# Delta-rule layer: output normalization gathered in the last slots, look-ahead of eleven slots in place of twelve

## The chip, the cores and the metric

The kernel runs on one core of a Trainium2 chip. Its engines are TensorE (PE, with its weight loads as PEld), VectorE (DVE), ScalarE (ACT), GpSimd (POOL) and SyncE (SP), which issues all the transfers spoken of here. The metric is the device time of one execution in microseconds (us); lower is better.

## What is computed

The reference is a chain of eight layers on a tensor x of shape 4 x 1024 x 128 (float32); each adds its result to x after a layer norm of its input. Only the first layer is touched, a delta rule with 8 heads of 16 dimensions:

```python
q = (x @ Wq).reshape(Bb, Ll, H, HD);  k = (x @ Wk).reshape(Bb, Ll, H, HD)
k = k / jnp.maximum(jnp.linalg.norm(k, axis=-1, keepdims=True), 1e-12)
v = jax.nn.silu(x @ Wv).reshape(Bb, Ll, H, HD)
beta = jax.nn.sigmoid(x @ Wb)
def step(S, inp):                       # over the 1024 tokens
    qt, kt, vt, bt = inp
    Sk = jnp.einsum('bhk,bhkv->bhv', kt, S)
    S = S + jnp.einsum('bh,bhk,bhv->bhkv', bt, kt, vt - Sk)
    ot = jnp.einsum('bhk,bhkv->bhv', qt, S)
    return (S, ot)
S0 = jnp.zeros((Bb, H, HD, HD), x.dtype)
_, os_ = jax.lax.scan(step, S0, (qs, ks_, vs, bs))
o = jnp.moveaxis(os_, 0, 1).reshape(Bb, Ll, Dd)
mu = jnp.mean(o, axis=-1, keepdims=True);  var = jnp.var(o, axis=-1, keepdims=True)
return (o - mu) / jnp.sqrt(var + 1e-05) * ln_w + ln_b
```

## The kernel before

`l0_attn` cuts the 1024 tokens into 32 chunks of 32 tokens (NS = 32, C = 32). A chunk holds the tokens of all four batches, so that its 4 x 32 rows fill 128 partitions. Within a chunk the recurrence is solved in closed form; from chunk to chunk a state S is carried. After a first part (layer norm and projections, which ends 49 us into the span) the work goes through a list of *slots* written out by hand: the loop `for slot in range(-LAG - 1, NS + 4)` issues, for chunk c = slot, a fixed sequence, and `tc.manual_schedule()` keeps that order on every engine. Each engine works through its own list in order; semaphores alone tie the lists together.

In slot c these steps are issued, in this order:

- the state applied to the chunk: matmuls into `up`, then ACT copies it to `ux` (L426, four instructions) and `uP` (L428);
- `gram(c + LAG)`: 8 pairs of Gram matmuls into `wide` (L277), ACT copies them to `kk` (L301), SP stores the diagonal blocks to DRAM (`ld`, L304), and for each fourth chunk SP loads the whole group of four chunks back as `L` (L307);
- `fetch(c + 2)`: SP loads the solved matrices `tb` from DRAM (`td`, L330);
- `root` (L396): the square root of an output tile's variance, on ACT;
- the state update: matmuls into `sp` (L437), ACT copies to the next `S` (L445);
- in two slots of four, one half of `query` for the next group (matmul L337, copy L341);
- `apply(c + 1)`: matmuls with `tb` into `wp` (L349), ACT copies to `wu` (L354);
- the first half of this slot's share of `solve`;
- the output matmuls `oT` (L457), ACT copy `ot`;
- `attend(c + 2)`: score matmuls into `wide` (L277) and on DVE one multiply with the causal mask, `mt<-wide,upper` (L366);
- the output: matmuls into `op`, ACT copy `o` (L474), SP stores it to DRAM as `od` (L475);
- `flip(c + LAG + 1)`: two POOL multiplies (L283, L284), four transposes (L288), two ACT copies `kt` and `bt` (L292, L294);
- the second half of this slot's share of `solve`;
- `reload`, `moments` and `norm` of an output tile, where one is due.

`solve(n)` is a forward substitution over a group of four chunks at a time (n = 0 to 7), on DVE: 31 steps of two instructions each (L319 `pr<-T,L`, L322 `T<-T,pr`), cut by PARTS into eight parts, two for each of four slots. `T` starts as a copy of `eye` on POOL (L313); after part 7 SP stores T to `td` (L324).

An output tile n is 128 tokens of all four batches, four chunks. `reload(n)` (SP load `on<-od` at L381, and on POOL the addition of `ln_b` to x at L382), `moments(n)` (on DVE 4 x `bn_stats` L390 and `bn_aggr` L391), `root(n)` and `norm(n)` (on DVE a reciprocal L401 and 4 x two fused instructions, L403 and L405) come four to seven slots after the tile's first chunk: `every(k)` gives the tile n in slot 4n + k, and is asked with 4, 6, 7 and 7. So before the change the DVE work of tile n falls into the slots 4n + 6 and 4n + 7, and LAG = 12 sets how far `flip`, `gram` and `solve` run ahead: with `n = (slot + 7) // 4` the four parts of solve(n) lie in the slots 4n - 7 to 4n - 4.

Two things tie DVE and PE to each other in each slot. The score matmuls of `attend` and the Gram matmuls both write `wide`, and the mask multiply reads it: the Gram matmuls of the next slot wait for this slot's mask multiply. And DVE, working in order, starts a mask multiply only after the solve instructions issued ahead of it.

Of the kernel before, what the change touches and what calls it, by code (L numbers as in the profile page):

```python
# [9 lines left out]
F32 = mybir.dt.float32  # L10
# [5 lines left out]
P = 128  # L16
NB, SEQ, D = 4, 1024, 128
TPB = SEQ // P
# [9 lines left out]
class Net:  # L28
# [112 lines left out]
    def l0_attn(self):  # L141
# [6 lines left out]
        nc, tc = self.nc, self.tc  # L148
        wkvb, wq, ln_w, ln_b = self.l0
        H, HD, C = 8, 16, 32  # L150
        NS, LAG = SEQ // C, 12
        PARTS = (0, 7, 11, 14, 16, 18, 21, 25, 31)
        mm = nc.tensor.matmul
        tok = self.xnT.rearrange("p (c r) -> p c r", r=P)
        with ExitStack() as c_:
            one = c_.enter_context(tc.tile_pool(name="dn1", bufs=1))
            two = c_.enter_context(tc.tile_pool(name="dn2", bufs=2))
# [55 lines left out]
            def heads(a):  # L213
                return a.rearrange("p (h d) -> p h d", h=H)
# [4 lines left out]
            with tc.tile_pool(name="dnl", bufs=NB) as ln, tc.tile_pool(name="dnp", bufs=3, space=PSUM) as pp_, tc.tile_pool(  # L219
                name="dnx", bufs=2, space=PSUM  # L220
# [76 lines left out]
            def gram(c):  # L297
                kt, bt = kT[c]
                sc = score(kt, bt, 0)
                kk = two.tile([P, H, P], F32, tag="kk", name="kk")  # L300
                nc.scalar.copy(kk.rearrange("p (j g) t -> p j g t", g=2), sc)  # L301
                for b in range(NB):
                    r = slice(C * b, C * b + C)
                    nc.sync.dma_start(ld[c, b].rearrange("h s t -> s h t"), kk[r, :, r])  # L304
                if c % 4 == 3:
                    Ls[c // 4] = L = two.tile([P, C, C], F32, tag="L", name="L")
                    nc.sync.dma_start(L, ld[c - 3 : c + 1].rearrange("c b h s t -> (c b h) s t"))  # L307
# [18 lines left out]
            def fetch(c):  # L326
                tb = tbs[c % len(tbs)]
                for b in range(NB):
                    r = slice(C * b, C * b + C)
                    nc.sync.dma_start(tb[r, :, r], td[c, b].rearrange("h s t -> s h t"))  # L330
# [26 lines left out]
            def with_state(out, w, g):  # L357

                for b in range(NB):
                    r = slice(C * b, C * b + C)  # L360
                    mm(out[r, g, :], lhsT=w[:, g, r], rhs=Ss[c % 2][:, g, b, :], start=True, stop=True)

            def attend(c):
                sc = score(kT[c][0], qs[c // 4][:, c % 4], 1)
                mt = two.tile([P, H, P], F32, tag="mt", name="mt", bufs=3)
                nc.vector.tensor_mul(  # L366
                    mt.rearrange("p (j g) t -> p j g t", g=2), sc,
                    upper.unsqueeze(1).unsqueeze(2).to_broadcast([P, 4, 2, P]),
                )
                del kT[c]  # L370
                return mt
# [3 lines left out]
            def of(n):  # L375
                return self.x.rearrange("p (b t) d -> p t b d", b=NB)[:, n]

            def reload(n):

                o = two.tile([P, NB, D], F32, tag="on", name="on")  # L380
                nc.sync.dma_start(o, od[:, n * P : (n + 1) * P, :].rearrange("b p d -> p b d"))  # L381
                nc.gpsimd.tensor_add(of(n), of(n), ln_b.unsqueeze(1).to_broadcast([P, NB, D]))  # L382
                outs[n] = [o]

            def moments(n):
                o = outs[n][0]
                mv = two.tile([P, NB, 2], F32, tag="mv", name="mv")
                for b in range(NB):
                    st = two.tile([P, 6], F32, tag="st", name="st", bufs=4)
                    nc.vector.bn_stats(st, o[:, b, :])  # L390
                    nc.vector.bn_aggr(mv[:, b, :], st)  # L391
                outs[n].append(mv)

            def root(n):
                rs = two.tile([P, NB], F32, tag="rs", name="rs")
                nc.scalar.activation(rs, outs[n][1][:, :, 1], AF.Sqrt, bias=self.eps)  # L396
                outs[n].append(rs)

            def norm(n):
                o, mv, rs = outs.pop(n)  # L400
                nc.vector.reciprocal(rs, rs)  # L401
                for b in range(NB):
                    nc.vector.scalar_tensor_tensor(o[:, b, :], o[:, b, :], mv[:, b, 0:1], ln_w, ALU.subtract, ALU.mult)  # L403
                    xs = of(n)[:, b, :]
                    nc.vector.scalar_tensor_tensor(xs, o[:, b, :], rs[:, b : b + 1], xs, ALU.mult, ALU.add)  # L405
# [3 lines left out]
            def every(k):  # L409

                n = (slot - k) // 4
                return (n,) if (slot - k) % 4 == 0 and 0 <= n < NS // 4 else ()

            for slot in range(-LAG - 1, NS + 4):
                c, part = slot, (slot + 7) % 4
                n = (slot + 7) // 4
                cut = (2 * part, 2 * part + 1) if 0 <= n < NS // 4 else ()
                if 0 <= c < NS:
                    mt = late.pop(c)
                    up = psm.tile([P, 2, 64], F32, tag="sm", name="up")  # L420
                    for g in range(2):
                        with_state(up, wus.pop(c) if g else wus[c], g)

                    ux = two.tile([P, 2, NB, 64], F32, tag="ux", name="ux")
                    for b in range(NB):
                        nc.scalar.mul(ux[:, :, b, :], up, nbb[:, b : b + 1])  # L426
                    u = ups[c % 2]
                    nc.scalar.mul(u[:, :, 0:HD], heads(up.rearrange("p g d -> p (g d)")), -1.0)  # L428
                if 0 <= c + LAG < NS:
                    gram(c + LAG)  # L430
                if 0 <= c + 2 < NS:
                    fetch(c + 2)
                for i in every(7):
                    root(i)
                if 0 <= c < NS:
                    for g in range(2):
                        mm(  # L437
                            sp[:, g].rearrange("p a b -> p (a b)"),
                            lhsT=kns[c % len(kns)][:, 4 * g : 4 * g + 4, :].rearrange("p a b -> p (a b)"),
                            rhs=ux[:, g].rearrange("p a b -> p (a b)"), start=False, stop=True, skip_group_check=True,  # L440
                        )
                    if c + 1 < NS:
                        for j in range(4):
                            r, d = slice(32 * j, 32 * j + HD), slice(HD * j, HD * j + HD)
                            nc.scalar.copy(Ss[(c + 1) % 2][r, :, :, d], sp[r, :, :, d])  # L445
                for g in range(2):
                    for i in every(g - 4):
                        query(i, g)
                if 0 <= c + 1 < NS:
                    wus[c + 1] = apply(c + 1)  # L450
                for i in cut[0:1]:
                    solve(n, i)
                if 0 <= c < NS:
                    oT = psm.tile([P, 2, P], F32, tag="sm", name="oT")
                    for g in range(2):
                        for j in range(4):
                            mm(  # L457
                                oT[32 * j : 32 * j + 32, g, :], lhsT=u[:, 4 * g + j, :], rhs=mt[:, 2 * j + g, :],
                                start=True, stop=True,
                            )  # L460
                    ot = two.tile([P, 2, P], F32, tag="ot", name="ot")
                    nc.scalar.copy(ot, oT)
                if 0 <= c + 2 < NS:
                    late[c + 2] = attend(c + 2)
                if 0 <= c < NS:
                    op = psm.tile([P, 2, 64], F32, tag="sm", name="op")
                    for g in range(2):
                        with_state(op, qs[c // 4][:, c % 4], g)
                        mm(
                            op[:, g, :], lhsT=ot[:, g, :], rhs=pick.rearrange("p j v -> p (j v)"),  # L470
                            start=False, stop=True, skip_group_check=True,
                        )
                    o = two.tile([P, D], F32, tag="o", name="o")
                    nc.scalar.copy(o, op.rearrange("p g d -> p (g d)"))  # L474
                    nc.sync.dma_start(od[:, c * C : (c + 1) * C, :], o)  # L475
                if 0 <= c + LAG + 1 < NS:
                    flip(c + LAG + 1)
                for i in cut[1:]:
                    solve(n, i)
                for i in every(4):  # L480
                    reload(i)
                for i in every(6):
                    moments(i)
                for i in every(7):
                    norm(i)

# [1169 lines left out]
```

## Time and profile before

| what | us |
|---|---|
| median of six runs (2816.16 to 2829.55) | 2821.89 |
| the profiled execution, its own time | 2817.83 |
| its span, first to last instruction | 2816.1 |
| first solve instruction (L319) on DVE | 69.6 |
| last solve instruction on DVE, slot 24 | 321.4 |
| first mask multiply (L366), slot -2 | 104.0 |
| last mask multiply, slot 29 | 349.7 |
| last chunk's output copied (L474), slot 31 | 364.5 |

The span is the time on the core; the execution's own time lies 1.7 us above it. The stretch of slots thus covers about the first eighth of the span; the seven layers behind it are not touched. In the trace a group of instructions has its busy time, the mean of one, and the idle time of the engine before it with what ended it. "A <- B" among waits means that A's engine sat idle until B ended.

### The profile page before, as it was taken

The page shows a single profiled execution, that of the slowest core. Times are in us where ns is not written, and L with a number is a line of the kernel's source. Part 1 is how long each engine was busy: PE and PEld are TensorE (multiplying, and loading weights), DVE is VectorE, ACT ScalarE, POOL GpSimd, SP SyncE. Part 2 cuts the span into 40 slices and gives each one's busy share as a digit, 9 for nine tenths or more (in the row PEclk, how much of TensorE's full clock was granted, in tenths as well). Part 3 has the DMA queues.
Part 4 walks back from the last instruction along what each step waited for, and adds up shares of the span by engine and source line. Part 5 has one row for each costly group of instructions (what it writes and reads, how often), then busy time and mean ns, then how long its engine had stood idle before and what let it go on. Part 6 is the DMA issues. An engine that isn't in the chain of part 4 may idle for free.

```text
span 2816.1 us, 51848 instructions
## 1 busy us (share of the span) xinstructions
PE 2552.0 (91%) x20320; PEld 1282.5 (46%) x20320; DVE 1831.1 (65%) x3857; ACT 1537.4 (55%) x3486; POOL 179.5 (6%) x301
## 2 busy tenths in 40 slices
PE   5678768999989959999999768999999999999977
PEld 4455535699985523333333343333333333333356
DVE  5999657467763666777676146777776776777134
ACT  4465466655554450665666650666666666666642
POOL 6111000000000000000000050000000000000001
PEclk8698868899998965999999865999999999999968
DMA  2233220000000000000100000000000000000000
GB/s 53 63 86 77 55 59 1 1 1 1 2 2 1 1 1 15 13 14 14 21 14 10 5 0 8 8 8 11 9 9 9 8 12 8 10 8 8 4 9 24
DMA packets 116468, 46.62 MB, mean 17 GB/s; under 512 B 88402, under 2 KB 110843, under 8 KB 116220
## 3 DMA queue, kind: packets, MB, share of 16 engines
q1 hardware_dynamic: 116220, 43.25, 7.8%
q8 instruction: 163, 2.67, 0.4%
q14 instruction: 85, 0.70, 0.1%
HBM read 16.95 MB, written 12.98 MB: 11 GB/s over the span
## 4 chain that ended last, share of the span: by engine, by line
PE 63%; DVE 3%; ACT 2%; POOL 1%; issue 1%; DMA 0%; SPq 0%; POOLq 0%; DVEq 0%; ACTq 0%
PE pb L1183 30%; PE po L1205 15%; PE pa L1158 6%; PE ep L975 2%; PE tp L120 2%; PE pp L1098 1%; PE gp L923 1%; PE bp L988 1%; DVE st L82 1%; ACT xn L109 1%; PE pv L1079 1%; PE op L617 0%; PE bp L986 0%; DVE mv L83 0%; PE rp L1576 0%
## 5 line engine op out<-in xcount | busy, mean ns | idle before, releaser
L1187 ACT ACTIVATE es<-pb 128x512 f32<-128x512 f32 x1536 | 836.2, 594 | 561.2 <-PE pb L1183 406.6
L1183 PE MATMUL pb<-q,k 32*128 32x512 f32 x3072 | 957.5, 642 | 0.7 <-ACT es L1187 0.7
L1158 PE MATMUL pa<-k,q 32*128 32x512 f32 x3072 | 913.2, 680 | 16.8 <-DMA q<-q 15.9
L1170 DVE TENSOR_REDUCE bm<-pa 128x2 f32<-128x1024 f32 x512 | 626.1, 1225 | 275.4 <-PE pb L1183 169.4
L1205 PE MATMUL po<-es,v 128*32 128x256 f32 (+1 forms) x5760 | 480.0, 405 | 0.0
L1183 PEld LDWEIGHTS pb<-q,k 32*128 32x128 f32 x3072 | 314.7, 184 | 347.4 <-ACT es L1187 189.0
L1166 DVE TENSOR_REDUCE bm<-pa 128x16 f32<-128x1024 f32 x256 | 312.7, 1222 | 107.3 <-PE pb L1183 60.6
L1205 PEld LDWEIGHTS po<-es,v 128*32 128x32 f32 x5760 | 114.2, 108 | 543.1 <-issue 510.5
L1158 PEld LDWEIGHTS pa<-k,q 32*128 32x128 f32 x3072 | 253.7, 193 | 94.4 <-DVE bm L1170 50.4
L120 PE MATMUL tp<-ident,xn 128*128 128x128 f32 x192 | 65.3, 439 | 56.3 <-ACT xn L109 50.5
L319 DVE TENSOR_TENSOR pr<-T,L 128x31 f32<-128x31 f32 (+15 forms) x248 | 91.5, 369 | 27.6 <-DMA L<-ld 20.6
L1212 DVE COPY oT<-po 128x512 f32<-128x512 f32 x48 | 32.8, 682 | 109.1 <-PE po L1205 109.1
L322 DVE TENSOR_TENSOR T<-T,pr 128x31 f32<-128x31 f32 (+15 forms) x248 | 92.5, 373 | 8.5
L109 ACT ACTIVATE xn<-x,nm,rs 128x128 f32<-128x128 f32 x224 | 89.4, 482 | 7.6 <-DVE nm L106 7.6
L984 DVE SCALAR_TENSOR_TENSOR x<-ep,g,x 128x128 f32<-128x128 f32 x160 | 55.2, 349 | 30.0 <-ACT sc L982 19.9
L120 PEld LDWEIGHTS tp<-ident,xn 128*128 128x128 f32 x192 | 34.4, 186 | 88.3 <-ACT xn L109 60.0
L277 PE MATMUL wide<-bt,kt 32*128 32x128 f32 x512 | 32.7, 387 | 45.6 <-DVE mt L366 29.6
L729 ACT ACTIVATE w<-tr,half 128x128 f32<-128x128 f32 x128 | 47.0, 367 | 48.0 <-PE tr L727 45.1
L82 DVE BATCH_NORM_STATS2 st<-x 128x6 f32<-128x128 f32 x256 | 65.3, 266 | 11.8 <-DMA x<-in_L_attn_x_dram 3.9
L704 ACT ACTIVATE a<-hp,wb 128x128 f32<-128x128 f32 x128 | 47.0, 367 | 40.9 <-PE hp L700 39.9
L975 PE MATMUL ep<-L_ffn_expert_w,xnT 128*128 128x512 f32 x128 | 68.4, 624 | 0.0
L1457 POOL MEMSET c<- 128x512 f32 (+1 forms) x2 | 2.3, 1171 | 1021.7 <-PE tp L120 1021.7
(442 smaller groups left out, 3570.4 us busy)
## 6 DMA issues: line engine op xcount, KB each, us to landing
ld<-kk SPq DMA_DIRECT2D x128, 32.0 KB
L<-ld SPq DMA_DIRECT2D x8, 512.0 KB
td<-T SPq DMA_DIRECT2D x8, 512.0 KB
tb<-td SPq DMA_DIRECT2D x128, 32.0 KB
md<-nt SPq DMA_DIRECT2D x192, 2.0 KB
q<-md SPq DMA_DIRECT2D x192, 2.0 KB
x<-in_L_attn_x_dram SPq DMA_DIRECT2D x4, 512.0 KB
od<-o SPq DMA_DIRECT2D x32, 64.0 KB
```

Of the source, the lines that this page charges most:

```text
L82: nc.vector.bn_stats(st, src[:, i, :])
L109: nc.scalar.activation(dst[:, i, :], src[:, i, :], AF.Identity, bias=nm[:, i : i + 1], scale=rs[:, i : i + 1])
L120: nc.tensor.transpose(tp[:, i, :], xn[:, 4 * q + i, :], self.ident)
L319: nc.vector.tensor_mul(pv, T[:, 0 : j + 1, j : j + 1].to_broadcast(sh), L[:, j : j + 1, j + 1 :].to_broadcast(sh))
L322: nc.vector.tensor_sub(T[:, 0 : j + 1, j + 1 :], T[:, 0 : j + 1, j + 1 :], pv)
L975: nc.tensor.matmul(ep.rearrange("p a b -> p (a b)"), lhsT=self.tok(t), rhs=ew[:, 4 * h : 4 * h + 4, :].rearrange("p a b -> p (a b)"), star ...
L1158: nc.tensor.matmul(pa[:, j % 2, :], lhsT=st["q"][r, i * P : (i + 1) * P], rhs=st["k"][r, n * 512 : (n + 1) * 512], start=True, stop=True,)
L1166: nc.vector.tensor_reduce(out[:, :, 1:9], pa.rearrange("p j (c s) -> p j c s", c=8), axis=AX.X, op=ALU.max)
L1170: nc.vector.tensor_reduce(out[:, :, n : n + 1], pa, axis=AX.X, op=ALU.max)
L1183: nc.tensor.matmul(pb, lhsT=st["k"][r, kc * P : (kc + 1) * P], rhs=st["q"][r, n * 512 : (n + 1) * 512], start=True, stop=True,)
L1187: nc.scalar.activation(es[turn][:, j, :], pb, AF.Exp, scale=scale)
L1205: nc.tensor.matmul(po[r, cols], lhsT=vring[b % 2][:, kc, 4 * g + j, :], rhs=es[:, j, cols], start=kc == 0, stop=True, skip_group_check=True,)
```

## The change

It moves the output steps of the tiles 0 to 6 from every fourth slot into consecutive slots at the end, and sets LAG to 11. `reloads` lists the slots of `reload`: 23 to 29 for the tiles 0 to 6, and 32 for tile 7; `moments` come one slot later, `root` and `norm` two slots later. The buffers `on` and `mv` get three copies in place of two. With LAG = 11 each `flip`, `gram` and `solve` part is issued one slot later as counted from its chunk: solve(n) lies in the slots 4n - 6 to 4n - 3. The ring `kn` and the buffers `kt` are one smaller (LAG + 3). The loop runs from slot -12 to 34 in place of -13 to 35.

```diff
-        NS, LAG = SEQ // C, 12
+        NS, LAG = SEQ // C, 11
...
-                o = two.tile([P, NB, D], F32, tag="on", name="on")
+                o = two.tile([P, NB, D], F32, tag="on", name="on", bufs=3)
...
-                mv = two.tile([P, NB, 2], F32, tag="mv", name="mv")
+                mv = two.tile([P, NB, 2], F32, tag="mv", name="mv", bufs=3)
...
-            for slot in range(-LAG - 1, NS + 4):
-                c, part = slot, (slot + 7) % 4
-                n = (slot + 7) // 4
+            reloads = [NS - TPB - 1 + i for i in range(TPB - 1)] + [NS]
+            for slot in range(-LAG - 1, NS + 3):
+                c, part = slot, (slot + 6) % 4
+                n = (slot + 6) // 4
...
-                for i in every(7):
-                    root(i)
+                if slot - 2 in reloads:
+                    root(reloads.index(slot - 2))
...
-                for i in every(4):
-                    reload(i)
-                for i in every(6):
-                    moments(i)
-                for i in every(7):
-                    norm(i)
+                if slot in reloads:
+                    reload(reloads.index(slot))
+                if slot - 1 in reloads:
+                    moments(reloads.index(slot - 1))
+                if slot - 2 in reloads:
+                    norm(reloads.index(slot - 2))
```

## Prediction

> **What bounds the kernel now.** I read the slices of the page first, then busy time by stretch, then DVE's waits, then DVE's timeline.
>
> ```profile
> PE   5678768999989959999999768999999999999977
> DVE  5999657467763666777676146777776776777134
> ```
>
> Each digit is 70 us. Only in slices 2 to 4 (70 to 281 us) is DVE the full engine, and there lie the slots. Elsewhere PE leads, and the change does not reach it. By stretch (window, its length, busy time and instruction count of PE, PEld, DVE, ACT, POOL, granted clock):
>
> ```profile
> 69.60:321.40 251.80, 192.75 (x2816) 133.70 (x2816) 231.92 (x608) 133.27 (x405) 33.41 (x50) 0.80 0.32 71
> 321.40:364.50 43.10, 34.03 (x549) 23.79 (x548) 13.83 (x39) 20.55 (x74) 0.00 (x0) 0.83 0.22 51
> ```
>
> DVE is busy 92% from the first solve instruction to the last, 32% after it. Its waits between 69 and 322 us:
>
> ```profile
> DVE pr L319 <- DMA L<-ld: 20.6, 1, 20.6
> DVE mt L366 <- PE wide L277: 2.8, 4, 1.4
> ```
>
> The first ended at 69.6. So in 252 us DVE waited 2.8 us: there the slots run at DVE's pace, and what leaves DVE there can shorten them, until PE and ACT lead. The next lines are DVE's, then POOL's (start, length):
>
> ```profile
> 131.65 1.37 DVE L319 TENSOR_TENSOR pr<-T,L 128x247 f32<-128x247 f32 x1
> ...
> 260.52 1.28 DVE L322 TENSOR_TENSOR T<-T,pr 128x175 f32<-128x175 f32 x1
> 261.73 1.21 DVE L366 TENSOR_TENSOR mt<-wide,upper 128x1024 f32<-128x1024 f32 x1
> 263.24 1.31 DVE L322 TENSOR_TENSOR T<-T,pr 128x192 f32<-128x192 f32 x1
> ...
> 260.26 4.07 POOL L382 TENSOR_TENSOR x<-x,L_attn_ln_b 128x512 f32<-128x512 f32 x3
> ```
>
> A solve instruction that runs beside POOL's addition of ln_b takes 1.3 us, 0.95 more than its like (0.42, 0.34 and 0.36 us). The mask multiply beside it keeps its 1.21.
>
> **The change part by part.** I write M(s) for the start of the mask multiply of slot s. In the trace M(2) = 135.0, M(6) = 166.9, M(10) = 201.0, M(14) = 234.8, M(18) = 269.7, M(22) = 301.2, M(25) = 323.3, M(29) = 349.7.
>
> *Norms leave.* One tile costs DVE 169.78 to 171.38 (moments) and 177.13 to 180.03 (norm), 4.5 us; tiles 1 to 4 cost 4.3 to 4.4. Five tiles lay ahead of 321.4: 21.7 us leave the full stretch. That is a gain only where DVE then still leads.
>
> *What is late next.* Between two mask multiplies DVE has 4+4, 6+8, 12+14 or 8+6 solve instructions: undisturbed 3.6, 5.8, 7.7 to 8.0 and 6.0 us, each plus 1.14 for the mask. PE's price is from the end of a mask multiply, which frees `wide`, to the end of the next scores. In slot 6 (159.29 to 162.89) it is 3.6 at full clock; in slot 10 (193.34 to 199.66) 6.3 at half. With the first half of a query it is 6.3 in slot 4, with the second 5.7 in slot 5; both at full clock, but starting 0.9 late from ACT's copies.
>
> LAG = 11 moves the solve parts one slot on: 4+4 falls into slots 0 mod 4, where the query makes PE slow, 6+8 into slots 1, 12+14 into slots 2, 8+6 into slots 3. One group of four slots after the change, mask to mask:
> - slot 3: DVE leads, 1.14 + 6.0, plus 0.7 for POOL's copy of `eye` (the copy at 133 us lengthened one solve instruction from 0.42 to 1.13) and 0.2 for the flip: 8.0;
> - slot 0: PE leads. Nearest rows 4.5 (slot 9, a query with `wide` just freed) to 6.3 (slot 4); slot 4 lost 0.4 of it to a late `tb` behind the L load, which moves to slot 1. I take 5.0: 1.22 + 5.0 = 6.2;
> - slot 1: PE leads, U + 4.86 as in slot 5 (151.15 to 156.01), where U, the start of `ux`, comes 2.2 after the scores. The L load now stands before its `tb`: from `kk` (137.2) to the use of `tb` (147.1) it took 10 us in slots 3 and 4, which here ends about 0.6 after the 5.8 of the U path. 1.22 + 6.4 = 7.6;
> - slot 2: DVE leads, 1.14 + 8.0: 9.1.
>
> Sum 30.9; a half clock in slot 0 or 1 adds 1 to 2 and shows in two of three groups before, mostly where DVE covers it. I take 31.5, bounds 30 to 34. Before, it was 33.7 (134.7 over four groups).
>
> *The stages.*
> 1. Up to slot 2. DVE starts solving at 69.6 as before: L comes from the same four Gram chunks. M(-2) now stands behind 62 + 14 solve instructions, not 90; that point was passed at 98.1, M(-2) was 104.0. Then 1.14 + 6.0, then 1.22 + 6.6 (PE's row of slot 0, at half clock), then 7.6 and 9.1: M(2) = 98.1 + 7.1 + 7.8 + 7.6 + 9.1 = 129.7. Gain 5.3.
> 2. Slots 3 to 18: 4 x 31.5 = 126.0, plus 1.6 in slot 18 (item 3), against 134.7. Gain 7.1.
> 3. Slots 19 to 22. POOL's eight additions were spread; now the built order has them in a row behind the last copy of `eye`, which waits for the store of T(5). That is M(17) + 1.1 + 3.5 + 3.1 (the last store of this kind was issued at 256.1, the copy started at 259.25), just ahead of M(18). Eight times 1.43 us from there: one addition and the copy hit slot 18 (1.6), one runs beside a mask multiply, six hit slot 19: 1.14 + 6.0 + 5.7 = 12.8. Slots 20 to 22: 7.2, 7.3, 8.8. Sum 36.1 against 31.5. Loss 4.6.
> 4. Slots 23 to 25: 7.1; 5.8 (PE); 1.14 + 2.6 + 1.6 + 3.2 = 8.5 (six solve instructions, moments(0), eight): 21.4 against 22.1. Gain 0.7.
> 5. Slots 26 to 29: slot 26 holds twelve solve instructions, moments(1), norm(0): 1.14 + 3.5 + 1.6 + 2.7 = 8.9. Then DVE's 1.14 + 4.3 = 5.4 a slot is below PE's 5.7 to 7.3 (slots 26 to 29 before), so the norms are covered: 5.5 + 6.2 + 6.4. Sum 27.0 against 26.4. Loss 0.6. If that cover were gone, each of seven slots would cost up to 5.4.
>
> `root` takes 0.3 us on ACT ahead of the S copies; these wait for `sp` anyway (1.0 us after `uP` in slot 25). Only in slot 26 are the moments late (6.2 after the mask), which holds the S copies, and slot 27 after them, less than DVE does. SP gains one reload a slot, 0.4 to 0.5 us of issue behind `od`; queued behind it is the next slot's fetch, needed a slot later. From slot 30 on nothing changes: tile 7 still waits for the last `od`, and the dropped slot was empty.
>
> Total 5.3 + 7.1 - 4.6 + 0.7 - 0.6 = 7.9. The profiled execution's 2817.8 becomes 2809.9; it lay 4.1 below the median, so the median 2821.9 becomes 2814.
>
> [...]
>
> **The rivals.**
> - *PE and ACT eat it all.* Half clock in both PE-led slots: slot 0 1.22 + 6.9 (6.3 and the query), slot 1 2.2 + 6.0 (slot 12, `ux` to scores): a group of 8.0 + 8.1 + 8.2 + 9.1 = 33.4, nearly as before. Stage 2 then loses 0.5, stage 3 another 2: 5.3 - 0.5 - 6.6 + 0.1 = 1.7 slower, 2824. For it: the granted clock is 0.50 from 46 to 114 us and again from 192.6 to 199.4, behind DVE-led slots. Against it: PE then waits less, and the clock was 0.95 from 151 to 183.
> - *The bottleneck simply leaves.* If slots 0 and 1 run at slot 6's 3.6 and its like, DVE leads everywhere: 23.0 + 4 x 1.14 + 1.5 for POOL = 29.1 a group, 9.6 more over stage 2: 2804; down to 2800 if the additions fall beside waits.
> - *T comes late: slower.* Between the end of solve(n) and `apply(4n)` there is a slot less, 8 us. After: solve ends at M(1) + 4.6, and slot 3 stays at DVE's pace if `apply` starts by M(3) - 1.8 = M(1) + 15.3: 10.7 us. The way is store 3.1, four issues 1.9, landing 1.8 (issue 99.7, last packet 101.5) to 3.5 behind an L load: 6.8 to 8.5. It decides above 10.7, each us then costing 8 for eight groups. SP in order could do that, `fetch` and everything behind it waiting for T. At 12.7: 16 - 8 = 8 slower, 2830. Against it: before, only 4.9 us of waits for `tb`.
>
> The clock rival has a rule behind it: the Trainium skill, TensorE: Matmul & The Clock Gate, section "Part 1: The HAM clock gate", halves the clock after an idle window of about 3.4 us. By it the shorter waits of PE would favour the faster outcomes; PE's waits of 3.3 (to 168.3) and 2.7 us (to 193.5), each with half clock behind it, agree roughly.
>
> **How the numbers follow.** Forecast 0.55; bottleneck leaves 0.2; PE and ACT eat it 0.15; T late 0.1. What a measurement of this kernel can tell from no change is 0.2%, 5.6 us. In the forecast's case I let the group lie anywhere from 30.0 to 32.5, a gain of 14 to 4; up to 32.1 it is over 5.6, 84% of the case: 0.46, and 0.2 from the bottleneck that leaves: faster 0.66. The other 0.09 and three quarters of PE and ACT, 0.11, fall within 0.2%: 0.2. T late and the rest: slower 0.14. The range runs from 2801, the lower end of the second rival, to 2824, the price of the first; T late and the far ends are left out.
>
> **What would show it.** Right: DVE waits of about 1.5 and 0.7 us ahead of the mask multiplies of slots 0 and 1 mod 4 and hardly any elsewhere; M(18) near 257 and the last solve near 319; eight L382 in a row with one solve instruction of 1.3 us each; L390 to L405 only after the mask multiply of slot 24. Wrong: M(18) above 264 (PE-led), waits of `wp` for `tb` over 2 us in slots 3 mod 4 (T late), or mask multiplies over 8 us apart from slot 27 on.

## The result, and the profile after

After the change the median is 2813.4 us (28 runs, 2802.74 to 2820.44), before it 2820.62 (60 runs, 2811.81 to 2829.55): ratio 0.9973, 95% interval 0.9965 to 0.9981, some 7.6 us faster by the ratio. The profiled execution has a span of 2808.1 in place of 2816.1. The forecast was 2814, faster.

The two slice rows of the page (70 us a digit) show DVE no longer full in slices 2 to 4 (8 in place of 9), and PE about as full as before (6, 8, 7 in place of 6, 7, 8):

```profile
PE   5687778999989959999999769999999999999967
DVE  5888866567654666667675246777776777777134
```

By stretch (window, its length, busy time and count of PE, PEld, DVE, ACT, POOL, then granted clock, DMA share, GB/s), from the first solve instruction to the last and from there to the last chunk's copy:

```profile
70.50:315.30 244.80, 187.46 (x2904) 130.27 (x2904) 215.53 (x533) 135.30 (x412) 33.36 (x50) 0.84 0.31 71
315.30:356.20 40.90, 32.73 (x461) 22.63 (x460) 28.93 (x110) 18.18 (x67) 0.00 (x0) 0.71 0.27 67
```

DVE has 75 instructions fewer in the first stretch and is busy 88% of it, not 92%; the second holds 71 more at a lower clock. DVE's waits from 69 to 316 us:

```profile
DVE pr L319 <- DMA L<-ld: 20.4, 1, 20.4
DVE mt L366 <- PE wide L277: 13.4, 9, 3.7
```

Mask multiplies now wait 13.4 us for PE's scores, not 2.8: PE leads in some slots. Two more places matter. First POOL's additions of ln_b, and DVE beside them (start, length):

```profile
252.40 10.83 POOL L382 TENSOR_TENSOR x<-x,L_attn_ln_b 128x512 f32<-128x512 f32 x8
```

```profile
256.31 0.34 DVE L319 TENSOR_TENSOR pr<-T,L 128x192 f32<-128x192 f32 x1
256.69 1.31 DVE L322 TENSOR_TENSOR T<-T,pr 128x192 f32<-128x192 f32 x1
258.04 1.33 DVE L319 TENSOR_TENSOR pr<-T,L 128x207 f32<-128x207 f32 x1
...
263.52 0.40 DVE L319 TENSOR_TENSOR pr<-T,L 128x231 f32<-128x231 f32 x1
```

Eight additions in a row. One runs beside the mask multiply, which keeps its 1.21; the other seven lengthen one solve instruction each to 1.3 us, two in slot 18 and five in slot 19, and the next takes 0.40 as soon as they end. Second, ACT in the last slots: the root (L396) waits for DVE's moments, and the copies to the next S (L447, L445 before) stand behind it:

```profile
316.96 0.30 ACT L396 ACTIVATE rs<-mv,eps 128x4 f32<-128x4 f32 x1 [3.36 <-DVE mv L391]
317.16 1.08 ACT L447 COPY S<-sp 16x128 f32<-16x128 f32 x4
```

The prediction's marks, M(s) being the start of slot s's mask multiply:

| | before | forecast | after |
|---|---|---|---|
| M(2) | 135.0 | 129.7 | 130.4 |
| M(18) | 269.7 | 257.3 | 255.2 |
| groups of four slots, 3 to 18 | 33.7 mean | 31.5 | 31.1, 30.7, 30.7, 32.3 |
| M(22) | 301.2 | 293.4 | 290.7 |
| M(25) | 323.3 | 314.8 | 310.7 |
| slots 26 to 29 | 26.4 | 27.0 | 31.9 |
| M(29) | 349.7 | 341.8 | 342.6 |

### The profile page after: what moved, and what is told of

Read it like the earlier page. It is cut to its first block, busy times and chain, and to the rows that moved or that the text cites. A ratio compares the mean times of both kernels' runs of the same rounds, so it can differ in the third digit from the quotient of the medians.

```text
span 2808.1 us, 51859 instructions
## 1 busy us (share of the span) xinstructions
PE 2546.8 (91%) x20320; PEld 1278.4 (46%) x20320; DVE 1831.7 (65%) x3857; ACT 1537.5 (55%) x3486; POOL 179.1 (6%) x300
## 4 chain that ended last, share of the span: by engine, by line
PE 63%; DVE 3%; ACT 2%; POOL 1%; issue 1%; DMA 0%; SPq 0%; POOLq 0%; DVEq 0%; ACTq 0%
PE pb L1185 30%; PE po L1207 15%; PE pa L1160 6%; PE ep L977 2%; PE tp L120 2%; PE pp L1100 1%; ACT xn L109 1%; PE gp L925 1%; PE bp L990 1%; DVE st L82 1%; PE pv L1081 1%; PE op L619 0%; PE rp L1578 0%; PE bp L988 0%; DVE mv L83 0%
## 5 line engine op out<-in xcount | busy, mean ns | idle before, releaser
L277 PE MATMUL wide<-bt,kt 32*128 32x128 f32 x512 | 30.4, 365 | 42.9 <-DVE mt L366 31.6
```

## The experiments

Each kernel was timed beside the kernel before. The stretch behind M(29) took 2459 to 2470 us in the profiled executions, with no order that follows the edits, so places are read from the marks, and times from the ratios. Slots are those of the kernel after unless said otherwise.

| kernel | median | ratio, interval | M(2) | M(22) | M(29) |
|---|---|---|---|---|---|
| norms_late | 2809.75 | 0.9961 (0.9949 to 0.9973) | 134.4 | 296.3 | 344.0 |
| lag_only | 2819.98 | 0.9993 (0.9981 to 1.0005) | 131.4 | 299.0 | 349.0 |
| no_add | 2802.88 | 0.9941 (0.9922 to 0.9959) | 130.0 | 284.4 | 334.7 |
| no_norms | 2806.02 | 0.9946 (0.9925 to 0.9968) | 129.3 | 289.3 | 333.9 |
| early_add | 2807.23 | 0.9946 (0.9925 to 0.9967) | 130.0 | 283.5 | 338.1 |
| mom_first | 2814.00 | 0.9968 (0.9952 to 0.9983) | 128.5 | 288.5 | 343.9 |
| query_early | 2813.12 | 0.9967 (0.9950 to 0.9983) | 131.1 | 293.2 | 346.0 |
| all3 | 2811.40 | 0.9956 (0.9939 to 0.9973) | 131.6 | 291.6 | 345.9 |
| root_late | 2810.56 | 0.9962 (0.9947 to 0.9976) | 129.9 | 290.1 | 342.7 |
| fetch_first | 2811.40 | 0.9957 (0.9939 to 0.9975) | 128.2 | 288.8 | 343.9 |
| combo11 | 2805.02 | 0.9943 (0.9924 to 0.9962) | 130.5 | 281.5 | 332.4 |
| combo12 | 2800.46 | 0.9924 (0.9906 to 0.9943) | 135.1 | 284.6 | 329.5 |

**Which half of the change makes the gain?** norms_late keeps the old look-ahead; lag_only has the old output steps, `every(4)`, 6, 7 and 7, with the new look-ahead.

```diff
 norms_late, against after:
-        NS, LAG = SEQ // C, 11
+        NS, LAG = SEQ // C, 12
-                c, part = slot, (slot + 6) % 4
-                n = (slot + 6) // 4
+                c, part = slot, (slot + 7) % 4
+                n = (slot + 7) // 4
 lag_only: the same lines the other way, against before
```

> One half of the change alone: output tiles normalized from slot 23 on, but the look-ahead of twelve and the solve parts where they were. Theory A (the two halves add, each by its own mechanism): the start gains nothing, M(2) = 135; a group of four slots is DVE's 12+14, 8+6 and 6+8 slots (9.1, 8.2, 6.9) and PE's 4+4 slot without a query (5 to 6), 29.3 to 30.5 in place of 33.7 before and 31.1 after, so 13 to 17 us over four groups; eight additions of ln_b in a row now meet only solve instructions, 7.6 lost, and the last slots lose 4 to 6 as after. Together 0 to 5 shorter than before: 2816 to 2821. Rival B (the gain of the change is the look-ahead; what the norms leave, PE and ACT fill): groups stay at 33 or more and the additions and the last slots cost 10: 2826 to 2832.

> The other half alone: look-ahead of eleven and solve parts one slot on, output tiles normalized every fourth slot as before. Theory A: M(2) = 130.4 as after (4.6 gained); then moments (1.6) fall into slots 3 mod 4 (7.9 + 1.6 = 9.5), the norm (2.7) into slots 0 mod 4 where PE leads (1.14 + 3.6 + 2.7 = 7.5 in place of 5.8), slots 1 and 2 stay at 7.7 and 9.0: a group of 33.7, as before. The end as before: 4 to 5 shorter, 2815 to 2817. Rival B (the look-ahead does it all): 2812 to 2814, groups at 31 to 32. Rival C (it gives nothing, the norms do it all): M(2) at 135, 2820 to 2822.

The norms make the gain: norms_late is 0.39% faster, lag_only cannot be told from no change: its start is theory A's, its time rival C's, and rival B falls in both runs. The two marks show why. The look-ahead of eleven does bring M(2) forward, by 3.6 (before to lag_only) and 4.0 (norms_late to after). At M(29) 0.7 and 1.4 of that are left. The rows from M(2) to M(22) and on to M(29), of norms_late and then of after:

```profile
134.39:296.25 161.86, 127.12 (x2135) 89.97 (x2134) 140.16 (x331) 98.38 (x307) 27.49 (x40) 0.92 0.32 73
296.25:344.04 47.79, 38.30 (x592) 26.22 (x590) 37.40 (x118) 23.54 (x85) 0.00 (x0) 0.83 0.31 73
```

```profile
130.37:290.66 160.29, 128.58 (x2137) 91.14 (x2138) 140.86 (x331) 98.45 (x306) 29.85 (x43) 0.91 0.33 74
290.66:342.62 51.96, 41.07 (x592) 28.25 (x590) 42.45 (x132) 23.63 (x85) 0.00 (x0) 0.74 0.31 71
```

DVE's work from M(2) to M(22) is the same 331 instructions. Behind M(22) the kernel with eleven has 14 more (132 against 118): the solve instructions that no longer stood ahead of M(-2). The stretch behind M(22) is 4.2 us longer for it. The other two pairs with eleven and twelve show 15 instructions more there, at other prices: 1.5 (before to lag_only) and 6.1 (combo12 to combo11, below). norms_late ran faster than expected (2809.75, expected 2816 to 2821), and the marks explain only a part of that: M(29) came 5.7 earlier, little more than the 0 to 5 forecast, where the ratio says 11. Its groups, 31.0, 30.4 and 31.9, were no shorter than expected (29.3 to 30.5); slots 23 to 25 gained 3.5 that the expectation had not counted, and slots 26 to 29 lost 2.8 in place of 4 to 6. The rest of the 11 is not in the slots of the profiled execution. The additions cost about as forecast (its group with slots 15 to 18 took 37.2). lag_only's two groups from M(6) to M(14) came out as summed (33.6 and 33.5 against 33.7), but the 3.6 us gained at the start did not stay.

**What do the eight additions cost, and can they be had free?** no_add leaves them out; early_add moves them into DVE's first wait.

```diff
 no_add:
-                nc.gpsimd.tensor_add(of(n), of(n), ln_b.unsqueeze(1).to_broadcast([P, NB, D]))
 early_add, the same line as shift(n):
+            for i in range(2):
+                shift(i)
             for slot in range(-LAG - 1, NS + 3):
...
                     flip(c + LAG + 1)
+                if slot == 1:
+                    for i in range(2, TPB):
+                        shift(i)
```

> After the change, with the eight additions of ln_b on POOL left out (the output then lacks ln_b in the first layer). It prices the burst in slots 18 and 19. Theory A (solve instructions beside an addition take 0.95 us more, DVE leads there): slot 18 is 1.6 shorter, slot 19 about 5, M(22) comes 6 to 7 earlier (284 in place of 290.7) and the end as much: 2806 to 2808. Rival B (PE, in the slots behind, gives it back): M(22) at most 3 earlier, 2811 to 2813.

> After the change, with the eight additions of ln_b issued early: two ahead of the slots, six behind the flip of slot 1, which POOL reaches at about 64 us, while DVE waits for the first L until 70.5. Nothing is left out. Theory A (the additions cost only where DVE reads SBUF beside them): M(22) comes as without additions, 284.4, later by at most 2 for one or two solve instructions beside the last of the six, and the end with it: 2802 to 2807. Rival B (POOL's flips lie on the path to the first L, and 2.9 us ahead of them move everything): first solve and M(2) 2 to 3 later than after, M(22) at 287 or later, 2806 to 2811.

Theory A both times up to M(22), which comes 6.3 earlier without the additions (no_add's output then lacks ln_b) and 7.2 earlier with them early; slot 19 takes 7.0 in place of 11.8. Behind M(22) they part: M(29) comes 7.9 and 4.5 earlier, and the median of no_add is 3 below its forecast range, that of early_add at the upper end of its own. POOL and DVE of early_add:

```profile
63.86 7.38 POOL L379 TENSOR_TENSOR x<-x,L_attn_ln_b 128x512 f32<-128x512 f32 x6
```

```profile
70.68 0.62 DVE L319 TENSOR_TENSOR pr<-T,L 128x31 f32<-128x31 f32 x1 [20.61 <-DMA L<-ld]
71.33 0.19 DVE L322 TENSOR_TENSOR T<-T,pr 128x31 f32<-128x31 f32 x1
```

Six additions end at 71.2 and lengthen a single solve instruction, by 0.43. Alone they take 1.23 each, beside DVE 1.35 (10.83 / 8). The Trainium skill, SBUF — State Buffer, section "Who interferes with whom", lets such a DVE instruction contend with a GpSimd instruction that reads SBUF; the trace agrees, and prices it at 0.95 per addition, less than the addition's whole length.

**What lengthened slots 26 to 29?** no_norms takes DVE's work away there; mom_first and root_late keep it and change what ACT waits for.

```diff
 no_norms: root, moments and norm for tile 7 alone
-                if slot - 2 in reloads:
+                if slot - 2 == NS:
 mom_first: moved
+                if slot - 1 in reloads:
+                    moments(reloads.index(slot - 1))
                 for i in cut[1:]:
                     solve(n, i)
 root_late: moved from ahead of the sp matmuls to behind attend
+                if slot - 2 in reloads:
+                    root(reloads.index(slot - 2))
                 if 0 <= c < NS:
                     op = psm.tile([P, 2, 64], F32, tag="sm", name="op")
```

> After the change, with moments, root and norm of the tiles 0 to 6 left out (the output then lacks these rows' normalized values), their reloads and additions kept. It asks what lengthened slots 26 to 29 (31.9 us against 26.4 before). Theory A (DVE's moments and norms beside the last solve parts hold ACT's roots, these hold the S copies, PE idles and gets half clock): without them slots 26 to 29 take 25 to 27, and slots 23 to 25 about 18.4 in place of 20.0: 2804 to 2808. Rival B (the reloads' transfers, or PE's own work at half clock): slots 26 to 29 stay above 30, 2810 to 2813.

> After the change, with the moments of a tile issued ahead of the second half of the slot's solve part in place of behind it; DVE's work is the same. It asks which half of theory A of the run without norms lengthens the last slots. Theory A (ACT's root waits for the moments and holds the S copies): the roots of slots 25 and 26 find their moments done, ACT's waits for mv (7.2 in all) fall under 1, slots 26 to 29 take 27 to 29 in place of 31.9, 2809 to 2811. Rival B (DVE's own 1.6 + 2.7 a slot is the price, whoever waits): slots 26 to 29 stay at 31 to 32, 2812 to 2814.

> After the change, with the root issued behind attend, ahead of the copy o, in place of ahead of the S copies; DVE's work and its order stay. The run with moments first only moved the stall one slot on, since ACT reaches the next slot's root before DVE has passed the mask. Theory A (the root holds the S copies, PE idles behind them and gets half clock): ACT's waits of L396 vanish (under 0.5), slots 26 to 29 take 27 to 29 in place of 31.9, slot 26 staying at 8.9 by DVE's own work: 2809 to 2811. Rival B (DVE's 4.3 a slot is the price by itself): slots 26 to 29 stay at 31 to 33, 2812 to 2815.

Without the output steps slots 26 to 29 take 26.0 and run at a granted clock of 0.87, with the transfers kept (no_norms, then after at the same four slots, one row each):

```profile
307.90:333.90 26.00, 19.64 (x341) 13.92 (x340) 7.95 (x18) 13.17 (x48) 0.00 (x0) 0.87 0.37 92
```

```profile
310.70:319.50 8.80, 6.96 (x96) 4.76 (x96) 8.07 (x31) 3.44 (x13) 0.00 (x0) 0.61 0.33 101
319.50:326.90 7.40, 6.08 (x86) 4.24 (x78) 5.24 (x20) 3.65 (x13) 0.00 (x0) 0.60 0.38 80
326.90:335.40 8.50, 7.18 (x96) 4.90 (x92) 5.16 (x19) 3.54 (x13) 0.00 (x0) 0.54 0.24 54
335.40:342.60 7.20, 5.88 (x96) 4.13 (x89) 5.18 (x18) 3.56 (x13) 0.00 (x0) 0.76 0.29 66
```

So 5.9 us are the output steps', not the reloads' transfers. mom_first did not take the root's wait away, it moved it one slot on; the roots of mom_first:

```profile
314.77 0.30 ACT L396 ACTIVATE rs<-mv,eps 128x4 f32<-128x4 f32 x1 [1.78 <-DVE mv L391]
323.90 0.30 ACT L396 ACTIVATE rs<-mv,eps 128x4 f32<-128x4 f32 x1 [4.28 <-DVE mv L391]
```

In these slots ACT reached the root before DVE had passed the mask multiply ahead of the moments. Slots 26 to 29 took 32.0 and the median is 2814.0, rival B's numbers, but since the waits stayed (6.1 in all) the run tells nothing between the theories. root_late does: ACT's waits for mv fall from 7.2 to 2.2, none of it ahead of an S copy, and slots 26 to 29 take 29.5: in these executions the stall's part is 2.4 of the 5.9, though slot 28 still has 9.0 at a clock of 0.50. Slot 26's 8.9, DVE's own work, stays as expected; that is 2.8 over the 6.1 of no_norms. The waits for mv did not fall under 0.5, and 29.5 lies between the two theories' ranges. Slot 24 took 7.7 there, not 4.7, behind PE at half clock, and M(29) is the same; the time, 0.9962 against 0.9973, does not tell the two kernels apart.

**What does PE lead with in slots 0 and 1?** query_early moves the query to slots 2 and 3; fetch_first puts SP's tb loads in front of the stores and the L load.

```diff
 query_early (and a third buffer qp):
-                    for i in every(g - 4):
+                    for i in every(g - 6):
 fetch_first:
+                if 0 <= c + 2 < NS:
+                    fetch(c + 2)
                 if 0 <= c + LAG < NS:
                     gram(c + LAG)
-                if 0 <= c + 2 < NS:
-                    fetch(c + 2)
```

> After the change, with the two halves of a query issued two slots earlier (in slots 2 and 3 mod 4, where DVE leads, and with a third buffer). Theory A (the query makes PE lead in slots 0 and 1): slots 0 fall from 5.8 to 4.7 to 5.2, slots 1 from 7.1 to 8.3 to about 7.0, groups from 30.7 to 28.8 to 29.6; M(22) 5 to 8 earlier, 2805 to 2809. Rival B (PE's clock or the late tb, not the query, makes them slow; PE that waits longer gets half clock): groups at 30.3 or more, 2811 to 2814.

> After the change, with fetch issued ahead of gram in a slot, so that SP puts the tb loads in front of the four stores and the L load. Theory A (in slots 1 mod 4, apply waits for the tb that stands behind the L load): slots 1 that took 7.8 to 8.3 take 7.1, PE's waits of wp for tb (8.7 in slots 2 to 22) fall under 2, groups without half clock 29.8 to 30, M(22) 2 to 4 earlier: 2810 to 2812. Rival B (the fetch of a new group waits for T in front of the stores, and kk, L and the copies behind them come late): slots 2 or 3 lengthen, 2813 to 2820.

The query is not what makes them slow: in query_early slots 0 keep 5.4 to 5.8 and slots 1 take 8.0 to 8.9. What holds slots 0 there at full clock was not settled. The wait for tb stays. In after PE sat idle for it 3.0 from 130 to 290 us (the 8.7 of the expectation above adds the waits of PE's weight loads, which overlap these). The longest of these, in slot 5 of after, and then the sum in query_early:

```profile
150.57 0.65 PE L349 MATMUL wp<-tb,vk 128*32 128x128 f32 x16 [1.18 <-DMA tb<-td]
```

```profile
PE wp L349 <- DMA tb<-td: 8.3, 5, 2.5
```

fetch_first takes it away (0.8 left, in slot 23), and slots 1 take 7.1 each time. In after they take 7.1 plus that wait (1.2, 0.6, 0.8 and none in slots 5, 9, 13 and 17): the chain of stores, L load and tb held them. But it does not hold them in every execution. no_norms, whose order is that of after up to slot 22, waited for no tb in slots 1 and took 7.1 in all four. Yet from M(2) to M(22) fetch_first takes 160.6, after 160.3 and no_norms 160.0. The groups of fetch_first alternate, 31.5 and 29.9, and the other 1.7 is in slots 0 of every second group, at half clock (no_norms has two such slots 0 too). Rows of fetch_first before and in one of them, slot 12 (197.5 to 205.0):

```profile
196.24:199.65 3.41, 1.07 (x33) 0.82 (x26) 3.27 (x7) 1.81 (x8) 0.00 (x0) 1.00 0.38 61
199.65:203.06 3.41, 3.41 (x6) 1.58 (x6) 2.49 (x6) 2.01 (x5) 0.94 (x2) 0.50 0.46 81
```

In after the half clock fell into slots 3, which DVE leads, and cost nothing; here it fell where PE leads. The time of fetch_first, 0.9957, has an interval that overlaps that of the change, so a gain of this edit alone is not shown.

**A version with the winners.** all3 has early_add, mom_first and query_early; combo11 has early_add, root_late and fetch_first; combo12 is combo11 with the look-ahead of twelve.

> After the change, with all three edits: early additions, moments ahead of the second half, queries two slots earlier. Theory A (each takes its own piece of DVE's path): M(22) near 278 (284.4 without additions, less 6), the last slots 27 to 29, the sum 2794 to 2801. Rival B (once one is gone the others are covered, PE leads at about 30 a group): 2802 to 2806, no better than the early additions alone.

> After the change, with early additions, late root and fetch first together. Theory A (each takes its own piece): M(22) at 280 to 282 (283.5 with early additions alone, less 2 to 3), slots 26 to 29 at 27 to 29, M(29) at 328 to 332 in place of 342.6: 2799 to 2803. Rival B (PE, at half clock where it waits longer, gives back most): M(29) at 334 or later, 2804 to 2808.

> The same three edits, with the look-ahead of twelve and the solve parts one slot earlier (the early additions behind the flip of slot 0). It asks whether the look-ahead of eleven is worth anything once the rest is right. Theory A (DVE's work between its first solve and its last is the same in both, and what eleven gains at the start it gives back behind the last solve): M(2) at 134.4, groups 29 to 30, M(22) at 281 to 284, slots 23 to 29 at 45 to 46, M(29) within 2 of the kernel with eleven, the times within 3 of each other. Rival B (the start is a gain that stays): M(29) 4 to 5 later than with eleven, 4 to 5 slower.

all3 missed both ranges: slots 13 and 14 took 10.5 and 10.6 under a long half clock (that the query in slot 14 is to blame was not tested), and M(2) to M(22) is 160.0 against 153.4 with the early additions alone. combo11 has the marks of theory A, but for M(29), 332.4, just past its range, and the time of rival B; its interval is nearly that of the early additions alone. combo12 is the fastest kernel here, 0.9924, its interval below that of the change, and M(29) lies 20.2 earlier than before. It starts 4.6 later than combo11 and ends 2.9 earlier: with the rest put right, the look-ahead of eleven is worth nothing or less, though the intervals of the two times overlap. combo12's rows from M(2) to M(22) and on to M(29) show the last stretch back at 118 DVE instructions:

```profile
135.12:284.60 149.48, 123.11 (x2116) 87.62 (x2116) 133.11 (x332) 95.43 (x300) 17.52 (x32) 0.94 0.35 79
284.60:329.51 44.91, 35.76 (x592) 24.67 (x592) 37.40 (x118) 24.30 (x88) 0.00 (x0) 0.89 0.34 80
```

## Why the prediction was right, step by step

The sum was 7.9, the marks give 7.1 at M(29) and 8.3 at the last chunk's copy. The direction and its main cause were right; that the size came out so close is luck. The gain of stages 2 to 4 was 4.8 more than forecast, stages 1 and 5 fell 5.6 short, and the two cancelled.

- *Norms leave, DVE led:* right, and it is the whole gain. No tile's work is left ahead of M(22), and norms_late alone gives all that the change gives.
- *Stage 1, 5.3:* measured 4.6, by the mechanism named. What failed is that the sum kept it: the prediction let stages 4 and 5 swallow the later solve instructions at almost no price. It is work put off, 14 DVE instructions, which come back behind M(22), where this kernel takes 4.2 longer than norms_late.
- *Stage 2, 7.1:* measured 9.9. Slots 2 and 3 took 9.0 and 7.9 as forecast; slots 0 took 5.8 to 6.0, not 6.2. In slots 1 the late tb behind the L load was the right cause for what exceeds 7.1 (7.1 to 8.3 around the 7.6 forecast), though not every execution shows it. The query, which the prediction charged to slot 0, is not what makes it slow.
- *Stage 3, loss 4.6:* measured 4.0. The additions over slots 18 and 19 are priced at 6.3 to 7.2 by no_add and early_add, against 1.6 + 5.7. The built order was the right source; two additions met solve instructions in slot 18 and five in slot 19, not one and six.
- *Stage 4, gain 0.7:* measured 2.1; slot 24 had no half clock in that execution. It had in early_add, mom_first, root_late and fetch_first, which took 22.8 to 23.4 for these three slots. So this gain is, in part at least, that execution's.
- *Stage 5, loss 0.6:* measured 5.5, the mis-sized term. "Only in slot 26 are the moments late (6.2 after the mask), which holds the S copies, and slot 27 after them, less than DVE does" failed: the roots waited 3.2 and 3.4 in a row, ahead of M(25) and M(26), and slots 26 to 28 ran at 0.54 to 0.61, where the prediction took PE's price of before, at 0.76 to 1.00. By the rows above PE sat idle no longer than without the output steps (5.8 against 6.4 in no_norms) but was busy longer, 26.1 against 19.6: the time is lost as PE work at the lower clock. root_late puts 2.4 of it down to the roots; why the clock fell for the rest stays open. Slot 28 took 8.5, so one of the prediction's own signs of being wrong, mask multiplies over 8 us apart from slot 27 on, did appear. The bound written there, 5.4 a slot if the cover were gone, was never near.
- *PE and ACT eat it all:* the groups of this kernel never reached its 33.4, and the granted clock from M(2) to M(22) rose from 0.87 to 0.91. Half clock costs 1.6 to 1.7 in a slot 0 (7.4 to 7.5 against 5.8 in no_norms and fetch_first), as in its price, but not in every group.
- *T late:* no slot 3 was lengthened by tb; PE waited 0.4 for it in slot 7, which took 7.9 all the same. (The 4.9 us of waits before, named against this rival, add PE's 1.4 and the weight loads' 3.5, which overlap.) In fetch_first, where SP waits for T in front of the stores, slots 2 and 3 still took 9.0 and 7.9.

## What to carry to other kernels

When an engine is the bound over a whole stretch, work that leaves the stretch shortens it; starting a consumer earlier by putting off some of the bound engine's work is a loan, and the place where it is paid back must be priced too. Before moving steps out of the critical part, ask what else an in-order queue then runs early or late with them: POOL's additions bunched in front of DVE, and ACT's root held the next state. Idle engines ahead of the stretch (here POOL, while DVE waited for its first data) are a cheap place for work whose inputs are already there: six additions there cost 0.43.

## What the runs showed of the hardware that was not expected

Half clock on PE comes in whole steps on a fixed grid. Read in quarter-microsecond windows, the half-clock stretches of after start at 133.28, 164.00, 194.72 and 225.44 and last 3.41 each; longer ones of this kernel last 6.83 or 13.65. All starts of one execution agree modulo 3.413 us (0.16 in after, 1.67 in fetch_first, 1.20 in combo12), so the grid's place differs from one execution to the next and a slot's time with it. The Trainium skill, TensorE: Matmul & The Clock Gate, section "Part 1: The HAM clock gate", has this as a free-running window of 3.413 us; the trace agrees. It asks for an idle window before the drop; here the two windows ahead of drops in after were not idle, PE being busy 1.23 and 1.22 us of 3.41 in them (the first and third row):

```profile
160.59:164.00 3.41, 1.23 (x24) 1.04 (x19) 3.24 (x8) 1.98 (x8) 0.00 (x0) 1.00 0.32 56
164.00:167.41 3.41, 2.98 (x36) 1.86 (x35) 3.20 (x7) 2.04 (x6) 2.11 (x3) 0.50 0.45 81
191.31:194.72 3.41, 1.22 (x22) 1.05 (x19) 3.24 (x8) 1.97 (x8) 0.00 (x0) 1.00 0.28 43
```

The drops in after lie 30.72 us apart, nine windows, and its groups last 30.70 and 30.70; fetch_first's pairs of groups last 61.4, eighteen windows. That a group settles on a multiple of the window, and so gives back small gains, fits these numbers and is argued only: no run changed the grid, and the groups of early_add, 29.9, 30.1 and 32.3, do not settle.
